# A four-layer graph network in one kernel: the product of probabilities and v is taken for four row tiles at once

## The chip, the cores and the metric

The kernel runs on one core of a Trainium2 chip. The metric is the time of one execution on the device in microseconds (us); lower is better. A core has five engines that work beside each other and wait for each other by semaphores: TensorE (PE in the profile: matrix products, weights are loaded by PEld beside the products), VectorE (DVE), ScalarE (ACT), GpSimd (POOL) and SyncE (SP), which here only issues DMA transfers. Each engine works through its own list of instructions in a fixed order.

## The reference

Inputs are 32 graphs of 512 nodes with 256 features each and a 512x512 adjacency matrix of zeros and ones. Four layers follow; each is `x = layernorm(x + layer(x))`, in fp32:

```python
# layer 0: attention with 8 heads of 32 columns, masked by adj
q, k, v = heads(x @ Wq + bq), heads(x @ Wk + bk), heads(x @ Wv + bv)
scores = where(adj > 0, q @ k.T / sqrt(32), -9e15)
x = layernorm(x + (softmax(scores) @ v) @ Wo + bo)
# layer 1: h = (1 + eps) x + adj @ x, two dense layers with relu
x = layernorm(x + relu(h @ W1 + b1) @ W2 + b2)
# layer 2: g = eps x + adj @ x, dense to 1024, rmsnorm, silu, dense back
x = layernorm(x + silu(rmsnorm(g @ W1 + b1) * w) @ W2 + b2)
# layer 3: normalised graph Laplacian of layernorm(x), softplus
xn = layernorm3(x) * gamma + beta
x = layernorm(x + softplus(xn @ W_self + (L @ xn) @ W_neigh))
```

## The kernel before

**Tiling.** A graph (a "batch", index b) has NT = 4 row tiles of 128 nodes and DC = 2 chunks of 128 features. The eight heads form two groups g of HPG = 4 heads, so that a group fills 128 rows of q and k transposed (qT, kT). `graph(b)` (L508) records every operation of one batch: which engine, a planned cost, what it reads, writes and holds. Nothing is issued while recording.

**Attention.** `qk(m)` (L693) computes qT and kT of one head group. `attend(g)` (L762) then goes over the four row tiles t. For each it computes the scores of four heads (L776, four small products in four strips of 32 rows of the array), adds the mask and takes the row minimum on DVE (L800), and takes the exponential on ACT (L814). The probabilities `pq` must be transposed before they can be multiplied with v. For batches after the first, DVE transposes 32x32 blocks in place (L850), four DMAs write the tile to a DRAM buffer `via` (L862, 256 KB each), and one DMA reads it back in the transposed arrangement as `pT` (L874, 1 MB). The first batch (`early`) transposes on PE instead. The product with v, called pv (L893), uses four strips of 32 columns of the array and adds into one PSUM bank `po_att`. It is one operation for two row tiles: after t = 1 and after t = 3, so two operations for a head group and four for a batch. There are three buffers for `pT` and four for `via`. After pv the sums are divided out (`normalise`, L946) and the output weights Wo are applied (`pair_sum`, L980, written `po<-wo,oT`).

**The other stages**, by the names that the profile shows: `ph` (L1170) is the product of adjacency and x, `pa` and `pg` (L1187) are the first dense layers of layer 1 and 2, `po<-w,aT` and `po<-w,gT` (L991) their second ones, `pz` (L1436) and `pa_l` (L1478) are layer 3. Between them stand layernorms, whose reciprocal root is a small POOL operation (L1044). Small bf16 or narrow products spread row factors: `pm_t` (L934), `pr_r` (L963), `pm` (L1281), `pb` (L1314).

**Buffers that the change touches.** x is loaded into its own tile `x_sb` (one buffer, L573); POOL then writes x plus the bias of Wo into `y_att` (L683), the tile of the residual (two buffers). `kT` holds both head groups (two buffers, L689). In layer 2, ACT squares each of eight chunks into `sq` (two buffers, L1263), which POOL adds up (L549).

**What sets the order of the work.** The order is planned before anything is issued. Class `Order` (L60) simulates all engines with the planned costs and, at each step, lets an engine take the operation with the smallest key among those that can start soon (`run`, L108). A key is `b * PERIOD` plus a due time: a mix of the earliest and the latest start (`LATE`) plus a constant for the stage (`LEAD`); the last batch's keys are shifted by `HASTE`. Choosing an operation that needs another division of the PE array ("whole", "row" for scores, "col" for pv) adds `TURN_DUE` to its key. So work of three or four batches is interleaved, and from the third batch on the order repeats with each batch. All DMAs are issued by SP in the planned order; a DMA that waits holds up those behind it.

Of the kernel before, what the change touches and what calls it, by code (L numbers as in the profile page):

```python
# [9 lines left out]
F32 = mybir.dt.float32  # L10
# [9 lines left out]
RMS_EPS = 1e-6  # L20
HEADS = 8

PERIOD = 65998
LEAD = {
    "adjT": 17900, "agg1": -34100, "agg2": -112800, "degree": 46800, "diag": 80200,
    "lap": -5300, "ln0": -81400, "ln1": -47100, "ln2": 88600, "ln3": -37200, "load": -92700,
    "move": 7000, "pv": 8000, "pz": 22200, "qk": 5800, "rinv": -8800, "rms": -91800,
    "scores": -5600, "silu": 57000, "softplus": -39900, "v": -32400, "w11": -49700,
    "w12": -36000, "w21": 10500, "w22": -22500, "wo": 21900, "x3T": -21500, "xT": 67600,
}  # L30


# [27 lines left out]
class Order:  # L60
# [9 lines left out]
    TABLE, TABLE_DUE = 1300, 9000  # L70

    TURN = {"whole": 93, "row": 290, "col": 150}
    TURN_DUE = 500
    LATE = 0.09
    HASTE = 137

    def __init__(self):
        self.ops = []
# [204 lines left out]
def kernel(  # L283
# [117 lines left out]
    def load_x(b, t):  # L401
        nc.sync.dma_start(t(), x[b].rearrange("(t p) d -> p t d", p=P))
# [105 lines left out]
    def graph(b):  # L508
# [13 lines left out]
        def pe(cost, fn, r, w, *hold, turn="whole"):  # L522

            op([("PE", cost, fn, {"turn": turn})], r, w, hold)
# [44 lines left out]
        def small(name, bufs=2, shape=None):  # L569
            return Buf(sb, shape or [P, NT], F32, "s_" + name, f"{name}_{b}", bufs)  # L570


        xs = Buf(sb, [P, NT, D], F32, "x_sb", f"x_{b}", 1)  # L573
        ad = Buf(sb, [P, NT, N], F32, "adj_sb", f"adj_{b}", 1)
        op(
            [("SP", 4000 if first else 8100, lambda: load_x(b, xs), {"issue": 1500 if first else 560, "lat": 300})],
            [], [(xs,)],
        )
        op(
            [("SP", 6000 if first else 8900, lambda: load_adj(b, ad), {"issue": 3000 if first else 560, "lat": 300})],  # L580
# [73 lines left out]
        if early:  # L654
            for c in range(DC):
                pt = bank("pt")

                def tr_x(c=c, pt=pt):
                    for t in range(NT):
                        nc.tensor.transpose(  # L660
                            pt[:, t * P : (t + 1) * P], xs[:, t, c * P : (c + 1) * P], ident
                        )

                pe(460, tr_x, [(xs,)], [(pt,), ("begun", c)], xT)
                evacuate(lambda c=c: xT[:, c, :], pt, [(pt,)], [(xT, c)])
        else:
            for q in range(4):
                op(
                    [("SP", 4900, lambda q=q: load_blocks(xT(), x[b], q), {"issue": 660, "lat": 300})],
                    [("begun", c) for c in range(DC)], [(xT, c, q) for c in range(DC)],  # L670
                )
            dve(
                1200,
                lambda: nc.vector.transpose(
                    xT().rearrange("p c i -> p (c i)"), xT().rearrange("p c i -> p (c i)")
                ),
                [], [(xT, c, q) for c in range(DC) for q in range(4)]
                + [(xT, c) for c in range(DC)],
            )
        y = tmp([P, NT, D], "y_att", 2)  # L680
        pool(
            2400,
            lambda: nc.gpsimd.tensor_tensor(y(), xs(), rows(bo_r), ALU.add),  # L683
            [(xs,), ("bo",)], [(y, t) for t in range(NT)],
        )


        qT = tmp([P, DC, N], "qT", 1)
        kT = tmp([P, DC, N], "kT", 2)  # L689
        v = tmp([P, NT, D], "v", 2)  # L690
        xTc = [(xT, c) for c in range(DC)]

        def qk(m):  # L693
            stage[0] = "qk"
            for w, w_k, dst, bias_c, bias_k, scale in (
                (wq, "wq", qT, bqs_c, "bqs_c", QK_SCALE),
                (wk, "wk", kT, bk_c, "bk_c", 1.0),
            ):
                pq = bank("pq")

                def mm(w=w, pq=pq):
                    for c in range(DC):
                        nc.tensor.matmul(  # L703
                            pq(),
                            lhsT=w[:, c, m * P : (m + 1) * P],
                            rhs=xT[:, c, :],
                            start=(c == 0),
                            stop=(c == DC - 1),
                        )

                pe(1720, mm, xTc + [(w_k,)], [(pq,)], dst)
                to = lambda dst=dst: dst[:, m, :]
                src = pq
                if dst is kT and not early:
                    to = lambda: kT[:, m, :].rearrange("p (a c s) -> p c a s", a=4, c=4)
                    src = lambda pq=pq: pq().rearrange("p (c a s) -> p c a s", a=4, c=4)
                col = bias_c[:, m : m + 1]
                either(
                    [(pq,), (bias_k,)], [(dst, m)],
                    (  # L720
                        750,
                        lambda to=to, src=src, col=col, scale=scale: nc.vector.tensor_scalar(
                            to(), src(), scalar1=scale, scalar2=col,
                            op0=ALU.mult, op1=ALU.add,
                        ),
                    ),
                    (
                        680,
                        lambda to=to, src=src, col=col, scale=scale: nc.scalar.activation(
                            to(), src(), AF.Identity, bias=col, scale=scale  # L730
                        ),
                    ),
                )
# [28 lines left out]
        def attend(g):  # L762
# [5 lines left out]
            for t in range(NT):  # L768
# [4 lines left out]
                def mm(t=t, sc=sc):  # L773
                    for j in range(HPG):
                        hp = slice(j * HD, (j + 1) * HD)
                        nc.tensor.matmul(  # L776
                            sc[:, j, :],
                            lhsT=qT[hp, g, t * P : (t + 1) * P],
                            rhs=kT[hp, g, :],
                            start=True,  # L780
                            stop=True,
                        )

                pe(
                    870, mm, [(qT, g), (kT, g)], [(sc, j) for j in range(HPG)], mx,
                    turn="row",
                )

# [33 lines left out]
                    )  # L822
                stage[0] = "move"

                pT = tmp([P, 4, HPG, NT, 32], "pT", 3)
                pTs.append(pT)
                if early:
                    for j in range(HPG):
# [18 lines left out]
                else:  # L847
# [7 lines left out]
                    )  # L855


                    via = Buf(dr, [4, 32, 4, HPG * NT * 32], F32, "via", f"via_{b}", 4)

                    def away(pq=pq, via=via):  # L860
                        for i in range(4):
# [18 lines left out]
                        [(via,)], [(pT, a) for a in range(4)],  # L880
                    )

                if t % 2 == 0:
                    continue
                stage[0] = "pv"
                two = [(t - 1, pTs[t - 1]), (t, pT)]

                def pv(two=two):

                    for t, pT, c in [(t, pT, c) for t, pT in two for c in range(NT)]:  # L890
                        for j in range(HPG):
                            h = g * HPG + j
                            nc.tensor.matmul(  # L893
                                po[j * HD : (j + 1) * HD, t * P : (t + 1) * P],
                                lhsT=v[:, c, h * HD : (h + 1) * HD],
                                rhs=pT[:, :, j, c, :],
                                start=(c == 0),
                                stop=(c == NT - 1),
                            )

                pe(
                    1780, pv,
                    [(pT, a) for _, pT in two for a in range(4)] + [(v, c) for c in range(NT)],
                    [(po,)], oT, turn="col",
                )

# [230 lines left out]
        x1 = y  # L1137


        def residual(xin, bias_r, bias_k):  # L1140
            r = tmp([P, NT, D], "y", 3)
            pool(
                2400,
                lambda: nc.gpsimd.tensor_tensor(r(), xin(), rows(bias_r), ALU.add),
                [(xin, t) for t in range(NT)] + [(bias_k,)], [(r, t) for t in range(NT)],
            )
            return r

# [49 lines left out]
        stage[0] = "agg1"  # L1198
        set_diagonal(self1, "self1")
        hT = aggregate(x1)  # L1200
        r1 = residual(x1, b12_r, "b12_r")
        set_diagonal(self2, "self2")
        stage[0] = "w11"
        aT = tmp([P, C1, N], "aT", 1)
# [31 lines left out]
        for m in range(C2):  # L1236
# [16 lines left out]
            if m == 0:  # L1253
                act(
                    630,
                    lambda m=m: nc.scalar.activation(ssq(), gT[:, m, :], AF.Square),
                    [(gT, m)], [(ssq,)],
                )
            else:
                sq = tmp([P, N], "sq", 2)  # L1260
                act(
                    630,
                    lambda m=m, sq=sq: nc.scalar.activation(sq(), gT[:, m, :], AF.Square),  # L1263
                    [(gT, m)], [(sq,)],
                )
                add_to(ssq, sq, 1280, 690, [(sq,)], [(ssq,)])
# [235 lines left out]
        for rt in row_tiles:  # L1502
# [6 lines left out]
            s_ = lambda part=part: sp[:, part]  # L1509
            z_ = lambda part=part: zy[:, part, 0:D]  # L1510
            x_ = lambda part=part: x3[:, part]
            act(cost, lambda s_=s_, z_=z_: nc.scalar.activation(s_(), z_(), AF.Abs), z0, spk)
            act(
                cost,
                lambda s_=s_: nc.scalar.activation(s_(), s_(), AF.Exp, scale=-1.0), [], spk,
# [75 lines left out]
```

## Time and profile before

The page gives shares of the whole span; the stretch that counts is the repeating one.

| | |
|---|---|
| median of 3 runs | 3356.13 us (3354.51 to 3359.38) |
| profiled execution, its own time | 3356.19 us |
| its span from first to last instruction | 3354.4 us (1.8 us lie around it) |
| granted TensorE clock, mean | 0.996 |
| one batch in the repeating stretch, 1496.98 to 1599.11 us | 102.13 us |
| busy in that stretch | PE 102.13, DVE 88.09, ACT 58.76, POOL 26.61 us; DMA share 0.81 |

A busy PE in this table means that a product was in flight or modelled to be; the starts of the products, not their modelled ends, tell how fast they follow each other. The idle time that a group of instructions shows is followed by what ended it. For a DMA the page gives the median from issue to landing.

### The profile page before, as it was taken

To read this page: it belongs to the slowest core of one execution; us is meant where nothing else is said; L and a number is where in the kernel's file an instruction comes from. 1 tells how busy PE (TensorE), PEld (TensorE's weight loads), DVE (VectorE), ACT (ScalarE), POOL (GpSimd) and SP (SyncE) were. 2 spreads that over 40 slices of the span, in tenths; PEclk is the share of its full clock that TensorE was granted. 3 is DMA by queue.
4 is the path that set the end of the run, shared out by engine and by line. 5 is a ranking of instruction groups with operands and counts; after the bars stand their busy time and mean duration, and the time that the engine had idled before them with its cause. 6 is when DMAs were issued, how large, how long until landed. Compare 5 with 4: busy or idle time off the path is not lost.

```text
span 3354.4 us, 55143 instructions
## 1 busy us (share of the span) xinstructions
PE 3305.2 (99%) x19624; PEld 1980.2 (59%) x19624; DVE 2823.6 (84%) x6412; ACT 1887.3 (56%) x3863; POOL 843.4 (25%) x610
## 2 busy tenths in 40 slices
PE   8999999999999999999999999999999999999997
PEld 5556655566565566565666655665655665556654
DVE  7878888888888888888888888888888888888855
ACT  6555565565655655655555655555656556556533
POOL 1222222322222322222222223222222222232221
PEclk9999999999999999999999999999999999999999
DMA  5878878778878787787787787787887887877820
GB/s 143 246 235 216 207 200 222 226 202 211 204 202 234 204 220 197 206 219 226 201 215 207 202 228 214 208 210 201 215 232 199 214 206 201 225 224 183 206 53 13
DMA packets 768195, 677.23 MB, mean 202 GB/s; under 512 B 540208, under 2 KB 592304, under 8 KB 736176
## 3 DMA queue, kind: packets, MB, share of 16 engines
q1 hardware_dynamic: 767920, 673.71, 76.5%
q8 instruction: 155, 2.54, 0.3%
q14 instruction: 120, 0.98, 0.1%
HBM read 380.52 MB, written 293.08 MB: 201 GB/s over the span
## 4 chain that ended last, share of the span: by engine, by line
PE 96%; DVE 1%; ACT 1%; DMA 1%; issue 0%; POOL 0%; SPq 0%; POOLq 0%; DVEq 0%; ACTq 0%
PE po L991 23%; PE ph L1170 13%; PE pg L1187 13%; PE sc L776 8%; PE po_att L893 7%; PE pz L1436 7%; PE pa_l L1478 7%; PE pa L1187 7%; PE pq L703 6%; PE pv L744 3%; ACT pq L814 0%; PE pr_r L963 0%; PE pb L1314 0%; DVE pq L800 0%; DMA via<-pq 0%
## 5 line engine op out<-in xcount | busy, mean ns | idle before, releaser
L814 ACT ACTIVATE pq<-pq,mx 128x512 f32<-128x512 f32 x1024 | 729.0, 714 | 333.3 <-DVE mx L800 265.7
L800 DVE CUSTOM_DVE_ANT_0 pq<-sc,bias 128x512 f32<-128x512 f32 x1024 | 664.3, 685 | 42.3 <-PE sc L776 23.7
L850 DVE STREAM_TRANSPOSE pq<-pq 128x2048 f32<-128x2048 f32 x248 | 567.9, 2296 | 6.4 <-ACT pq L814 6.4
L1187 PE MATMUL pg<-hT,w 128*128 128x512 f32 x1024 | 480.3, 603 | 2.0 <-DVE gT L1242 2.0
L991 PE MATMUL po<-w,gT 128*128 128x256 f32 x2048 | 451.3, 381 | 6.3 <-ACT gT L1341 6.3
L991 PEld LDWEIGHTS po<-w,gT 128*128 128x128 f32 x2048 | 391.3, 191 | 62.1 <-ACT gT L1341 7.1
L549 POOL TENSOR_TENSOR ssq<-ssq,sq 128x512 f32<-128x512 f32 x217 | 276.9, 1276 | 521.6 <-ACT sq L1263 521.2
L1187 PEld LDWEIGHTS pg<-hT,w 128*128 128x128 f32 x1024 | 184.6, 190 | 251.0 <-issue 238.1
L776 PE MATMUL sc<-kT,qT 32*128 32x512 f32 x2048 | 291.9, 640 | 3.0 <-DVE mx L800 3.0
L893 PEld LDWEIGHTS po_att<-pT,v 128*32 128x32 f32 x8192 | 216.3, 110 | 99.1 <-issue 49.2
L893 PE MATMUL po_att<-pT,v 128*32 128x128 f32 x8192 | 251.2, 275 | 5.5 <-DMA pT<-via 5.5
L1478 PE MATMUL pa_l<-zy,adjT 128*128 128x256 f32 x1024 | 243.0, 385 | 0.0
L1044 POOL TENSOR_TENSOR rstd<-ve,nhalf 128x4 f32<-128x4 f32 (+1 forms) x132 | 135.6, 1028 | 422.5 <-DVE ve L1039 417.5
L1242 DVE TENSOR_SCALAR gT<-pg,b_c 128x512 f32<-128x512 f32 x187 | 140.3, 751 | 120.0 <-PE pg L1187 119.9
L549 POOL TENSOR_TENSOR sp<-sp,y 128x1024 f32<-128x1024 f32 x31 | 73.4, 2367 | 657.7 <-ACT sp L1528 644.7
L1436 PE MATMUL pz<-wsn,xnT 128*128 128x512 f32 x512 | 236.9, 606 | 0.7 <-ACT sq L1263 0.6
L1170 PE MATMUL ph<-adjT,y 128*128 128x512 f32 x512 | 227.0, 596 | 4.7 <-ACT y L1070 4.7
L1170 PE MATMUL ph<-adjT,y_att 128*128 128x512 f32 x512 | 228.2, 598 | 0.0
L1187 PE MATMUL pa<-hT,w 128*128 128x512 f32 x512 | 228.1, 598 | 0.0
L991 PE MATMUL po<-w,aT 128*128 128x256 f32 x1024 | 226.5, 379 | 0.0
L991 PEld LDWEIGHTS po<-w,aT 128*128 128x128 f32 x1024 | 194.3, 190 | 28.0 <-ACT aT L1218 0.8
L1478 PEld LDWEIGHTS pa_l<-zy,adjT 128*128 128x128 f32 x1024 | 189.3, 190 | 29.9 <-issue 0.7
(165 smaller groups left out, 4896.3 us busy)
## 6 DMA issues: line engine op xcount, KB each, us to landing
via<-pq SPq DMA_DIRECT2D x992, 256.0 KB, 4.4
pT<-via SPq DMA_DIRECT2D x248, 1024.0 KB, 6.4
adj<-in_adj_dram SPq DMA_DIRECT2D x32, 1024.0 KB, 7.9
adjT<-in_adj_dram SPq DMA_DIRECT2D x124, 256.0 KB, 6.0
x<-in_x_dram SPq DMA_DIRECT2D x32, 512.0 KB, 6.1
xT<-in_x_dram SPq DMA_DIRECT2D x124, 128.0 KB, 5.9
x3d<-y SPq DMA_DIRECT2D x31, 512.0 KB, 3.9
xnT<-x3d SPq DMA_DIRECT2D x124, 128.0 KB, 3.7
```

The source lines that it names most:

```text
L549: lambda: nc.gpsimd.tensor_tensor(dst(), dst(), src(), ALU.add), {},
L703: nc.tensor.matmul(pq(), lhsT=w[:, c, m * P : (m + 1) * P], rhs=xT[:, c, :], start=(c == 0), stop=(c == DC - 1),)
L776: nc.tensor.matmul(sc[:, j, :], lhsT=qT[hp, g, t * P : (t + 1) * P], rhs=kT[hp, g, :], start=True, stop=True,)
L800: lambda t=t, j=j, sc=sc, row=row: nc.vector.tensor_tensor_reduce(out=row(), in0=sc[:, j, :].rearrange("p (a n) -> p a n", a=4), in1=bias[ ...
L814: lambda t=t, j=j, row=row: nc.scalar.activation(row(), row(), AF.Exp, bias=mx[:, t, j : j + 1], scale=-1.0, accum_out=rs[:, g, t, j : j + 1],
L850: lambda pq=pq: nc.vector.transpose(pq().rearrange("p a j c s -> p (a j c s)"), pq().rearrange("p a j c s -> p (a j c s)"),),
L893: nc.tensor.matmul(po[j * HD : (j + 1) * HD, t * P : (t + 1) * P], lhsT=v[:, c, h * HD : (h + 1) * HD], rhs=pT[:, :, j, c, :], start=(c == 0),
L991: nc.tensor.matmul(po[:, i * D : (i + 1) * D], lhsT=lhs[:, k, t * P : (t + 1) * P], rhs=w[:, k, :], start=(i == 0 and k == 0), stop=(i == ...
L1170: nc.tensor.matmul(ph(), lhsT=xin[:, m, c * P : (c + 1) * P], rhs=adjT[:, m, :], start=(m == 0), stop=(m == NT - 1),)
L1187: nc.tensor.matmul(pa(), lhsT=w[:, c, m * P : (m + 1) * P], rhs=hT[:, c, :], start=(c == 0), stop=(c == DC - 1),)
L1436: nc.tensor.matmul(pz(), lhsT=xnT[:, c, t * P : (t + 1) * P], rhs=wsn[:, c, :], start=(c == 0), stop=(c == DC - 1),)
L1478: nc.tensor.matmul(pa[:, i * D : (i + 1) * D], lhsT=adjT[:, m, t * P : (t + 1) * P], rhs=zy[:, m, D : 2 * D], start=(m == 0), stop=(m == N ...
```

## The change

The product of probabilities and v becomes one operation for all four row tiles of a head group, recorded after the last of them (t = 3). It needs all four `pT` tiles at once, so there are four `pT` buffers, and eight `via` buffers. To make room, x is loaded straight into `y_att`, where POOL adds the bias in place; `x_sb` is gone; `kT` becomes one tile for each head group with three buffers; `sq` has one buffer. Two keys are added that order operations only in the plan: the residual of layer 1 comes after the softplus of two batches before. The constants of the plan (period, leads, price of a turn) are other ones, so that the order of the work changes everywhere.

```diff
-PERIOD = 65998
+PERIOD = 63146
 LEAD = {
...
-    TURN_DUE = 500
-    LATE = 0.09
-    HASTE = 137
+    TURN_DUE = 1750
+    LATE = 0.17
+    HASTE = -6727
...
-        xs = Buf(sb, [P, NT, D], F32, "x_sb", f"x_{b}", 1)
+        y = tmp([P, NT, D], "y_att", 2)
...
-            [("SP", 4000 if first else 8100, lambda: load_x(b, xs), {...})],
-            [], [(xs,)],
+            [("SP", 4000 if first else 8100, lambda: load_x(b, y), {...})],
+            [], [(y, t) for t in range(NT)],
...
-        y = tmp([P, NT, D], "y_att", 2)
         pool(
             2400,
-            lambda: nc.gpsimd.tensor_tensor(y(), xs(), rows(bo_r), ALU.add),
-            [(xs,), ("bo",)], [(y, t) for t in range(NT)],
+            lambda: nc.gpsimd.tensor_tensor(y(), y(), rows(bo_r), ALU.add),
+            [("bo",)], [(y, t) for t in range(NT)],
         )
...
-        kT = tmp([P, DC, N], "kT", 2)
+        kTs = [tmp([P, N], "kT", 3, f"kT{g}") for g in range(DC)]
...
-                            rhs=kT[hp, g, :],
+                            rhs=kTs[g][hp, :],
...
-                pT = tmp([P, 4, HPG, NT, 32], "pT", 3)
+                pT = tmp([P, 4, HPG, NT, 32], "pT", 4)
...
-                    via = Buf(dr, [4, 32, 4, HPG * NT * 32], F32, "via", f"via_{b}", 4)
+                    via = Buf(dr, [4, 32, 4, HPG * NT * 32], F32, "via", f"via_{b}", 8)
...
-                if t % 2 == 0:
+                if t < NT - 1:
                     continue
                 stage[0] = "pv"
-                two = [(t - 1, pTs[t - 1]), (t, pT)]
-
-                def pv(two=two):
-
-                    for t, pT, c in [(t, pT, c) for t, pT in two for c in range(NT)]:
+
+                def pv():
+
+                    for t, c in [(t, c) for t in range(NT) for c in range(NT)]:
                         for j in range(HPG):
                             h = g * HPG + j
                             nc.tensor.matmul(
                                 po[j * HD : (j + 1) * HD, t * P : (t + 1) * P],
                                 lhsT=v[:, c, h * HD : (h + 1) * HD],
-                                rhs=pT[:, :, j, c, :],
+                                rhs=pTs[t][:, :, j, c, :],
...
                 pe(
-                    1780, pv,
-                    [(pT, a) for _, pT in two for a in range(4)] + [(v, c) for c in range(NT)],
+                    3500, pv,
+                    [(pT, a) for pT in pTs for a in range(4)] + [(v, c) for c in range(NT)],
                     [(po,)], oT, turn="col",
                 )
...
-        r1 = residual(x1, b12_r, "b12_r")
+        r1 = residual(x1, b12_r, "b12_r", [("sp", b - 2)])
...
-                sq = tmp([P, N], "sq", 2)
+                sq = tmp([P, N], "sq", 1)
...
-            act(cost, lambda s_=s_, z_=z_: nc.scalar.activation(s_(), z_(), AF.Abs), z0, spk)
+            act(
+                cost, lambda s_=s_, z_=z_: nc.scalar.activation(s_(), z_(), AF.Abs), z0,
+                spk + [("sp", b)],
+            )
```

## The prediction

> **What bounds the kernel now.** I read the page's engine shares and its chain first, then PE's own waits, then PE's timeline in a repeating stretch. The page:
>
> ```profile
> PE 3305.2 (99%) x19624; PEld 1980.2 (59%) x19624; DVE 2823.6 (84%) x6412; ACT 1887.3 (56%) x3863; POOL 843.4 (25%) x610
> PE 96%; DVE 1%; ACT 1%; DMA 1%; issue 0%; POOL 0%; SPq 0%; POOLq 0%; DVEq 0%; ACTq 0%
> L893 PE MATMUL po_att<-pT,v 128*32 128x128 f32 x8192 | 251.2, 275 | 5.5 <-DMA pT<-via 5.5
> pT<-via SPq DMA_DIRECT2D x248, 1024.0 KB, 6.4
> ```
>
> PE is busy for 99% of the span and 96% of the chain that ended last lies on it. Does it ever wait? The list of PE's waits:
>
> ```profile
> PE po L991 <- ACT gT L1341: 6.3, 2, 4.8
> PE po_att L893 <- DMA pT<-via: 5.5, 1, 5.5
> PE ph L1170 <- ACT y L1070: 4.7, 2, 2.7
> PE pt L1379 <- DVE y L1062: 4.3, 1, 4.3
> ```
>
> Each occurs once or twice in 32 batches: at the start or in the last two batches. In the repeating stretch PE waits for nothing, one batch takes 102.13 us, and the time is what PE needs to issue its list. So only a shorter list, or a new wait, moves the time. What a piece costs is read from start to start, not from the modelled durations:
>
> ```profile
> 1568.99 1.88 PE L703 MATMUL pq<-xT,wk 128*128 128x512 f32 x4
> 1570.71 1.88 PE L1187 MATMUL pg<-hT,w 128*128 128x512 f32 x4
> 1572.52 1.14 PE L776 MATMUL sc<-kT,qT 32*128 32x512 f32 x8
> 1573.59 5.42 PE L1187 MATMUL pg<-hT,w 128*128 128x512 f32 x12
> 1578.94 1.96 PE L893 MATMUL po_att<-pT,v 128*32 128x128 f32 x64
> 1580.82 5.42 PE L1436 MATMUL pz<-wsn,xnT 128*128 128x512 f32 x12
> 1586.08 0.29 PE L1281 MATMUL pm<-red,quad 128*128 128x16 f32 x2
> ```
>
> Four whole products of 512 columns take 1.72 us (1568.99 to 1570.71), so 0.429 each; four that precede scores take 1.81: 0.09 more. The twelve between scores and pv take 5.35 instead of 5.15, and the twelve after pv 5.26. So one visit to the divided array costs 0.20 us beside its own work: 0.09 going in, 0.11 coming back. Scores that are followed at once by pv take 1.07 us all the same, so a pair costs 0.20 once. A pv of two row tiles takes 1.88 us. What of that is start-up shows near the beginning, where one is cut in half by a wait:
>
> ```profile
> 151.54 1.08 PE L893 MATMUL po_att<-pT,v 128*32 128x128 f32 x32
> 158.13 1.94 PE L893 MATMUL po_att<-pT,v 128*32 128x128 f32 x32 [5.51 <-DMA pT<-via]
> ```
>
> 32 products have the duration 1.08 and 64 have 1.96, so 32 more cost 0.88.
>
> **The change, part by part.** Counts are from the instruction order of the changed kernel, which can be listed without running it; PE has the same 10566 program instructions in both.
>
> *Pv in one operation.* 128 operations become 64. One of four tiles takes 1.88 + 2 x 0.88 = 3.64 us against 2 x 1.88 = 3.76: 0.12 saved, 64 x 0.12 = 7.7 us.
>
> *Fewer visits to the divided array* (pv merged, dearer turn, new leads). Unbroken runs of scores and pv fall from 295 to 258: 37 x 0.20 = 7.4 us. In a repeating batch it is nine against eight.
>
> *Small products at new places.* `pm` now stands before scores in 28 batches; before, it stood between two `pz`, and took 0.14 us to issue with the four `pz` after it 0.08 slow. `pm_t` of the sums now precedes scores in 30 batches, against `pg` 0.05 slow after it before. If scores hide all of that, 28 x 0.19 + 30 x 0.06 = 7.1 us go; if their turn costs come on top, nothing. The nearest row, `pm_t` before scores near the start (0.14 from start to start), shows it half hidden; I take 3.5. Work of PE: -18.6 us, between -15.1 and -22.2.
>
> The Trainium skill ("TensorEngine Tiling (Array Packing)", Key Properties) says that changing the tiling mode drains TensorE, but not a change of tile alone. The trace shows 0.20 for a visit and no visible extra between scores and pv, two different modes. By the rule every such pair would have a third drain; at 0.1 each, 28 pairs fewer (88 to 60) would add some 3 us to the gain.
>
> *Four `pT` held until pv ends.* No load of the next group's `pT` can land earlier: what is late next is the four loads that SP issues after a pv. Summing PE's prices in the new order, the second pv of a batch stands 19.0 us after the end of the first (pz, scores, `po<-wo`, `pa_l`, scores). What do four loads need? Two issued 0.9 us apart (1.23 less one issue of 0.34) land after 6.2 and 7.8 us, 2.5 apart:
>
> ```profile
> 1544.28 1.23 SPq L874 DMA_DIRECT2D pT<-via  x2
> DMA to landing us min/median/max: 6.2/7.0/7.8
> DMA to landing us min/median/max: 4.6/6.4/9.9
> ```
>
> (The last line is over all 248.) So 0.3 + 6.4 + 3 x 2.5 = 14.2 us; with the longest landing 17.7. Spare: 4.8, at worst 1.3 us. Cost 0. If the cover goes, PE stands and with it everything, once in each batch. The `via` writes are done in time: scores of that group lie 30 us or more ahead. The other pv comes 75 us after its predecessor.
>
> The Trainium skill ("Trainium Kernel Development and Optimization", Best Practices) asks for double buffering, so that transfers run beside compute. It speaks against this: a fourth buffer that is consumed with the other three leaves none to load ahead. By it the loads would be exposed; by the rows 19.0 us of other products cover them.
>
> *At the start* that cover is missing: between the pv of the second batch stand only 6.4 us of PE, against 14.2: a wait of 7.8 us, where before there was one of 5.5: +2.3.
>
> *x into `y_att`.* Same bytes, same POOL operation (2.38 us). The load now waits on SP for PE and POOL to let go of `y_att` of two batches before, at the end of the first aggregation; the queue behind it holds `via` and `pT` transfers needed over 20 us later. Landing takes 6.1 us and the addition 2.4; behind it in POOL's list stands the root of layer 1's layernorm, asked for about 20 us after the load can start: spare 11 us. Cost 0; if that cover were gone, PE would wait for the second aggregation.
>
> *`kT` by group, `sq` with one buffer.* A `kT` tile is written again some 80 us after the last scores that read it: 0. A square (0.63) and its addition on POOL (1.28) can no longer overlap, 2.1 us with two hand-overs for each of seven chunks, where `pg` come every 1.72 plus two or three scores between them. The chain ends some 2 us later; `pm` comes 10.2 us after the last `pg` instead of 7.2: 0. The two order keys add no instruction and no wait of their own.
>
> *New order, new slacks.* Tightest is layernorm 1, from the last `po<-w,aT` to the second `ph`. Before, 6.6 us of PE covered it and the normalised rows were ready 0.9 us early. Now 6.4 us cover it (three `pq`, `pm_t`, scores), and DVE first does three masks and a 2.3 us transpose of probabilities. Summing DVE's list from the start of that `po` (reductions until 2.6, masks 4.2, reciprocal 4.4, transpose 6.7, two additions 7.9, statistics 10.2, root on POOL 11.5, two rows 12.4) against 13.3 leaves 0.9 us. The same sum for the transposed adjacency (four loads landed 9.6 us after `pa_l` ends) leaves 1.4 us. Cost 0, bound 0.5 for a batch. DVE's total falls by some 9 us in the run, since more copies went to ACT.
>
> *At the end* layernorm 1 of the last but one batch is covered by `pm_t` and `pr_r` alone (0.5 us) instead of scores and pv (2.96): its wait of 1.94 becomes 4.4, +2.4. From the first aggregation of the last batch on, the order is the same.
>
> Sum: -18.6 + 2.3 + 2.4 = -13.9 us. Against the profiled execution's 3356.2 (its own time; the median is 3356.1, the same) that is **3342 us**.
>
> **Rivals.** A: small recurring waits. Layernorm 1 or the adjacency misses its slack by 0.2 to 0.5 us in 29 repeating batches: +6 to +15, so 3348 to 3357. For: slacks of about a microsecond on a DVE that is 86% busy. Against: before ran with 0.9 and no wait.
>
> B, the other side: `pT` loads late for the second pv. It decides from where four loads take 19.6 us instead of 14.2 (the spare 4.8 and some 0.6 saved in a batch), that is 4.3 us from one to the next instead of 2.5. At the mean rate of the run (202 GB/s, 5.2 us for 1 MB) they would take 22.3: 3.3 us of stall, x 29 = +96, 3438 us. For: DMA share 0.81. Against: loads issued together follow at 2.5 us even so.
>
> C: no change that counts. Turns are saved but PE waits for them elsewhere, since another engine or the loop from batch to batch holds 102.1: 3354 to 3358. Against: DVE, the next, needs 88 of 102.
>
> **How the numbers follow.** Forecast 72%; its own range takes work of -15 to -22 and start and end waits of 0 to +9: 3333 to 3350. A 14%, B 7%, C 4%, a wait that I have not seen 3%. The range 3333 to 3353 takes in most of A. About 0.2% (6.7 us) is what a measurement tells from no change, so faster is below 3349.4: the forecast and half of A, 0.79. Same: half of A and C, 0.11. Slower: B and the unseen, 0.10.
>
> **What would show it.** One batch near 101.6 us; 64 pv groups of 128 products, 3.6 us from start to start; PE's list of waits still made of single events, with `po_att` near 8 us at one place; `ph` after layernorm 1 without a recurring wait. Wrong: `po_att <- pT` or `ph <- ACT y` some 29 times, or a batch of 102.1 us with a new idle engine before PE.

## The result and the profile after

| | before | after |
|---|---|---|
| median | 3355.56 us | 3401.3 us (3398.24 to 3405.35) |
| ratio | | 1.0135, 95% interval [1.0117, 1.0153] |
| span of the profiled execution | 3354.4 us | 3400.9 us |
| granted TensorE clock, mean | 0.996 | 0.993 |

The change makes the kernel slower by 46 us; 14 us less was forecast. The lines of the page that answer to those shown of the kernel before:

```profile
PE 3305.0 (97%) x19624; PEld 1992.9 (59%) x19624; DVE 2751.4 (81%) x6338; ACT 1897.9 (56%) x3936; POOL 843.0 (25%) x610
PE 69%; DMA 12%; SPq 11%; DVE 5%; issue 2%; ACT 1%; DVEq 0%; POOL 0%; POOLq 0%; ACTq 0%
L895 PE MATMUL po_att<-pT,v 128*32 128x128 f32 x8192 | 238.3, 274 | 4.6 <-DMA pT<-via 4.6
pT<-via SPq DMA_DIRECT2D x248, 1024.0 KB, 7.8
```

PE fell from 99% of the span to 97%. The chain that ended last no longer lies on PE alone: 28% of it is transfers, SP's queue and DVE. A `pT` load lands after 7.8 us in the median instead of 6.4. Who makes PE wait is in the list of PE's waits (total us, times, longest us):

```profile
PE pv L747 <- DVE xT L677: 27.3, 24, 2.8
PE sc L779 <- DVE mx L803: 9.2, 5, 5.2
PE ph L1172 <- issue: 7.5, 25, 2.1
PE po_att L895 <- DMA pT<-via: 4.6, 3, 3.0
PE pz L1438 <- DVE gT L1244: 4.2, 1, 4.2
```

The first and the third come in most batches, once in each: the products that make v (`pv<-wv,xT`, not the pv of this change) wait for the transposed x, and `ph` behind them again. The list of before has no line of this kind. The wait for `pT` at the second pv of a batch, rival B, is absent: 4.6 us in three events, all near the start.

Where the 46.5 us of span lie, by the starts of the first `ph` of each batch (us):

| stretch | before | after | difference | by the forecast's terms |
|---|---|---|---|---|
| to the fourth batch | 393.0 | 406.7 | +13.7 | about +1 |
| one of the next 26 batches | 102.13 | 103.39 | +1.26 | -0.6 |
| these 26 | 2655.5 | 2688.2 | +32.7 | -15 |
| the rest | 305.9 | 305.9 | 0 | about +1 |

The chain of one repeating stretch says what stands behind the wait. Its pieces in order of time (start us, us, what):

```profile
1709.17 3.68 PE po_att L895 x128
...
1713.59 9.13 DMA pT<-via
1722.71 0.02 issue
1722.73 5.61 SPq L590
...
1728.39 2.20 SPq L590
...
1735.23 7.37 DMA adjT<-in_adj_dram
...
1745.10 2.19 DVE pq L853
1747.29 1.14 DVE xT L677
1748.42 0.04 issue
1748.47 3.72 PE pv L747 x16
```

A pv ends and lets go of four `pT` at once. Four loads of 1 MB start between 1712.36 and 1716.01 us; a `via`, xT of a later batch and the transposed adjacency (both L590) follow. The last load of the adjacency lands at 1742.60. For 3.95 us until then DVE stands, with the transposes of probabilities and of xT behind it in its list. DVE and PE in that stretch (the bracket is the idle time before, and what ended it):

```profile
1742.72 2.37 DVE L624 STREAM_TRANSPOSE adjT<-adjT 128x1024 f32<-128x1024 f32 x2 [3.95 <-DMA adjT<-in_adj_dram]
1745.02 2.27 DVE L853 STREAM_TRANSPOSE pq<-pq 128x2048 f32<-128x2048 f32 x1
1747.21 1.20 DVE L677 STREAM_TRANSPOSE xT<-xT 128x1024 f32<-128x1024 f32 x1
```

```profile
1727.05 3.72 PE L1480 MATMUL pa_l<-zy,adjT 128*128 128x256 f32 x16
1730.70 1.14 PE L779 MATMUL sc<-kT,qT 32*128 32x512 f32 x8
1735.72 12.03 PE L993 MATMUL po<-w,gT 128*128 128x256 f32 x55
1748.47 3.72 PE L747 MATMUL pv<-wv,xT 128*128 128x256 f32 x16 [0.71 <-DVE xT L677]
1752.42 4.10 PE L1172 MATMUL ph<-adjT,y_att 128*128 128x512 f32 x9 [0.23 <-issue]
```

The adjacency's tile comes free when `pa_l` ends (1730.8). Before, its last load landed 10.2 us after that (median of 25 batches, 9.3 to 11.1); after the change 12.1 us (10.8 to 13.9). The delay is there already when the loads are started: the last of the four starts 6.0 us after `pa_l` ends instead of 4.0, and from its start to its landing it takes 6.2 us against 6.1 (medians). SP's rows for xT and the adjacency, first before, then after:

```profile
1693.12 4.30 SPq L589 DMA_DIRECT2D xT<-in_x_dram  x3
1700.26 5.52 SPq L589 DMA_DIRECT2D adjT<-in_adj_dram  x4
```

```profile
1720.29 11.01 SPq L590 DMA_DIRECT2D xT<-in_x_dram  x4
1731.40 6.96 SPq L590 DMA_DIRECT2D adjT<-in_adj_dram  x4
```

Part of that is a wait of SP's own. Each transfer raises one of eight semaphores when it has landed, and the four loads of xT have the same four semaphores as the four of `pT` ahead of them: an xT load is not started before its `pT` load has landed (the second one landed at 1722.71, and the second xT load starts at 1722.73). From 400 to 3000 us SP's list of waits has this line; that of before has none like it:

```profile
SPq L590 <- DMA pT<-via: 62.3, 46, 3.3
```

The windows of the changed kernel (busy time of each engine, then granted clock, DMA share, GB/s) show what the transfers do meanwhile:

```profile
1720.00:1724.00 4.00, 4.00 (x20) 3.51 (x20) 3.83 (x12) 2.78 (x9) 0.00 (x0) 1.00 1.03 422
1736.00:1740.00 4.00, 4.00 (x20) 3.54 (x19) 2.78 (x9) 3.95 (x6) 0.00 (x0) 1.00 1.20 116
```

From 1712 to 1744 us the DMA share is 1.02 in the mean: the transfer engines are busy through the whole stretch, first with `pT` at 422 GB/s, then with the adjacency in pieces of 128 bytes at 116. (The share is reckoned from the packets' own times and can pass 1.)

### The profile page after: what moved, and what is told of

It reads as the page before. It is cut to its first block, busy times and chain, and to the rows that moved or that the text cites. A ratio compares the mean times of both kernels' runs of the same rounds, so it can differ in the third digit from the quotient of the medians.

```text
span 3400.9 us, 54937 instructions
## 1 busy us (share of the span) xinstructions
PE 3305.0 (97%) x19624; PEld 1992.9 (59%) x19624; DVE 2751.4 (81%) x6338; ACT 1897.9 (56%) x3936; POOL 843.0 (25%) x610
## 4 chain that ended last, share of the span: by engine, by line
PE 69%; DMA 12%; SPq 11%; DVE 5%; issue 2%; ACT 1%; DVEq 0%; POOL 0%; POOLq 0%; ACTq 0%
PE ph L1172 13%; PE pg L1189 13%; PE po L993 10%; SPq L590 10%; PE pq L706 6%; DMA pT<-via 6%; PE sc L779 6%; PE pa L1189 6%; DMA adjT<-in_adj_dram 4%; PE po_att L895 4%; PE pz L1438 4%; PE pv L747 3%; PE pa_l L1480 2%; DVE pq L853 2%; DVE adjT L624 1%
## 5 line engine op out<-in xcount | busy, mean ns | idle before, releaser
L803 DVE CUSTOM_DVE_ANT_0 pq<-sc,bias 128x512 f32<-128x512 f32 x1024 | 654.3, 682 | 39.0 <-PE sc L779 23.3
L1189 PE MATMUL pg<-hT,w 128*128 128x512 f32 x1024 | 460.7, 598 | 0.0
L895 PE MATMUL po_att<-pT,v 128*32 128x128 f32 x8192 | 238.3, 274 | 4.6 <-DMA pT<-via 4.6
L1328 DVE SCALAR_TENSOR_TENSOR gT<-gT,rw_c,pb 128x512 f32<-128x512 f32 x256 | 171.3, 742 | 35.0 <-PE pb L1316 35.0
L817 ACT ACTIVATION_READ_ACCUMULATOR pq<-pq,mx 128x1 f32 x1024 | 191.9, 187 | 0.0
```

What stands on the lines that cost most here:

```text
L803: lambda t=t, j=j, sc=sc, row=row: nc.vector.tensor_tensor_reduce(out=row(), in0=sc[:, j, :].rearrange("p (a n) -> p a n", a=4), in1=bias[ ...
L817: lambda t=t, j=j, row=row: nc.scalar.activation(row(), row(), AF.Exp, bias=mx[:, t, j : j + 1], scale=-1.0, accum_out=rs[:, g, t, j : j + 1],
L895: nc.tensor.matmul(po[j * HD : (j + 1) * HD, t * P : (t + 1) * P], lhsT=v[:, c, h * HD : (h + 1) * HD], rhs=pTs[t][:, :, j, c, :], start=( ...
L1189: nc.tensor.matmul(pa(), lhsT=w[:, c, m * P : (m + 1) * P], rhs=hT[:, c, :], start=(c == 0), stop=(c == DC - 1),)
```

## The experiments

Theory T1 after the first look: the four loads that one pv sets free crowd the transfers, the adjacency lands late and DVE hands the wait on. Rivals: T2, DVE's list is too long there, whatever the transfers; T3, PE's own products cost more in the new order.

**1. The same loads in long rows.** xT and the transposed adjacency are loaded in rows of 4 and 8 KB instead of pieces of 128 bytes: the same bytes, the same operations behind them.

```diff
...
-    load_blocks(adjT(), adj[b], q)
+    load_plain(adjT(), adj[b], q)
...
-    load_blocks(xT(), x[b], q)
+    load_plain(xT(), x[b], q)
```

> The changed kernel with the rows of xT and of the transposed adjacency loaded as they lie (packets of 4 and 8 KB) instead of gathered in blocks (packets of 128 B): same bytes, same order, same instructions. The arrangement of x and adjacency for the products is left out, so the values are others. Theory T1 (the adjacency lands late for VectorE, because the burst of four pT loads, via, xT and the adjacency go through one queue at the same time): the wait of pv on the transposed xT goes, a batch takes 101.5 to 101.8 us, the span is 3355 to 3368. Rival T2 (VectorE's list from the Laplacian to the second aggregation is too long, whatever the loads do): the wait stays, a batch keeps 103.4 and the span 3395 or more. Rival T3 (PE's own list is dearer than its prices say): waits go, a batch still takes over 102.5.

Measured: 3352.41 us (one run; the kernel before on the same chip 3357.51). A batch takes 101.65 us in the mean of 26, and from 400 to 3000 us PE's list of waits is empty. T1 holds: with cheaper transfers the waits go, and DVE's list and PE's order are as they were, so T2 and T3 fall. The adjacency now lands 7.5 us after `pa_l` ends (median, 6.7 to 8.8).

PE's list is the same here as in after, instruction by instruction, so the two can be laid on each other. Over the 26 batches after takes 45.3 us more, and all of it lies in three places: 31.1 in front of `pv<-wv,xT`, 5.6 between its products, 8.7 between it and `ph`. Everything else differs by hundredths of a microsecond. This kernel also shows PE's prices without a wait:

```profile
1680.96 3.70 PE L901 MATMUL po_att<-pT,v 128*32 128x128 f32 x128
1684.59 3.70 PE L1444 MATMUL pz<-wsn,xnT 128*128 128x512 f32 x8
1688.13 0.29 PE L1289 MATMUL pm<-red,quad 128*128 128x16 f32 x2
1688.35 1.14 PE L785 MATMUL sc<-kT,qT 32*128 32x512 f32 x8
```

A merged pv takes 3.63 us from start to start; 3.64 was forecast. `pm` before scores takes 0.22, as much as its 0.14 and 0.08 before: scores hide nothing of it.

**2. Half of each pT.** Each `pT` load brings half of the tile, and pv takes one of its four blocks four times.

```diff
-    pT().rearrange("p i j c s -> p (i j c s)"), via().rearrange("a p i e -> (a p) (i e)")
+    pT()[:, 0:2].rearrange("p i j c s -> p i (j c s)"), via()[:, :, 0:2].rearrange("a p i e -> (a p) i e")
...
-    rhs=pTs[t][:, :, j, c, :]
+    rhs=pTs[t][:, 0:1, j, c, :].to_broadcast([P, 4, 32])
```

> The changed kernel with half of each pT loaded (512 KB instead of 1 MB), and pv reading one of the four blocks four times: same products, other values; half of the probabilities' way back is left out. T1 with the burst as the cause: the four loads take 5 us of the queue instead of 10, the adjacency lands some 2 us or more earlier, the wait of pv on xT goes, a batch takes 101.5 to 102, the span is 3355 to 3375. T2: no change, 3395 or more.

Measured: 3359.71 us (one run), 102.06 us for a batch, the adjacency 10.8 us after `pa_l`. So the bytes of `pT` count, and not only the pieces of 128 bytes. This kernel moves fewer of them everywhere, not in the burst alone; that their timing matters, and not their sum, follows from the kernel before, which moves as many as after. Kernels 1, 2 and after have the same order of work, so their batches can be laid on one curve: from the end of `pa_l` to the landing of the adjacency, and from the same end to the next `ph` (us, from the records of single batches):

| kernel | landing -> `ph` |
|---|---|
| long rows | 6.7 -> 20.4; 7.7 -> 20.4; 8.8 -> 20.4 |
| half of pT | 10.0 -> 20.4; 10.6 -> 20.4; 11.0 -> 20.8; 12.0 -> 21.8 |
| after | 10.8 -> 20.6; 11.9 -> 21.7; 12.4 -> 22.2; 12.9 -> 22.7; 13.8 -> 24.6 |

PE reaches `ph` after 20.4 us as long as the adjacency lands within 10.6; beyond that each microsecond costs a microsecond. Two of the 25 batches of after lie about 1 us above that line, the last one of the table among them. In both the granted TensorE clock stood at half for 3.4 us from the products behind the wait on (0.72 in the window from 1540 to 1546 us), which the repeating batches of the kernel before and of kernels 1 and 2 never show.

**3. xT's transpose ahead of the adjacency's on DVE.** In 23 batches DVE transposes xT, which has long landed, before it waits for the adjacency.

```diff
...
+            if ad and 6 <= b < 29:
+                out.remove(tr[0])
+                out.insert(ad[0], tr[0])
...
```

> The changed kernel with one VectorE instruction moved in 23 of the batches: the transpose of xT stands before that of the adjacency, where VectorE is idle for 4 us. T1: xT has landed some 9 us before the adjacency, so pv no longer waits for it, and what hangs on the adjacency is 1.1 us shorter: a batch takes 101.6 to 102.2, the span is 3365 to 3380. T2: the same work is only done in another order, the second aggregation waits instead: 3390 or more.

Measured: 3378.76 us, ratio 1.0062 [1.0046, 1.0079]; a batch 102.43 us, a little over what T1 gave it. The adjacency lands as late as in after (median 12.0). More than half of the loss in a batch goes; what stays has moved one product on, by PE's waits from 400 to 3000 us:

```profile
PE ph L1203 <- ACT v L573: 10.3, 7, 1.9
PE ph L1203 <- issue: 2.9, 9, 0.6
PE pv L778 <- DVE xT L708: 2.6, 3, 1.1
```

**4. xT's loads ahead of the burst.** As 3, and SP issues the four xT loads before the last `via` and the four `pT` loads.

```diff
...
+                for o in ld:
+                    out.remove(o)
+                j = out.index(before)
+                out[j:j] = ld
...
```

> As the kernel with the moved transpose, and the four loads of xT ahead of the last via before the burst of pT loads, where SP idles. T1: the small packets of xT are out of the way when the adjacency is issued, which lands 1 to 3 us earlier; a batch takes 101.5 to 101.7, the span is 3360 to 3370, some 10 us better than the moved transpose alone at most. T2: no better than the moved transpose alone. If the burst of pT alone delays the adjacency, no better either.

Measured: 3614.93 us, ratio 1.0768 [1.0752, 1.0784]: a miss, far off. The waits of SP's queue from 700 to 3000 us, and those of PE, name it:

```profile
SPq L621 <- PE pz L1469: 286.6, 21, 13.7
```

```profile
PE pa_l L1511 <- ACT zy L1496: 173.5, 21, 9.2
```

The tile of xT comes free only at `pz`, so SP stands up to 13.7 us in front of these loads, and the `via` behind them starts late. The reductions wait for that `via` (a `pq` buffer), and `pa_l` in the end for ACT. In each of the 23 batches the granted clock also fell to half for 10.2 us (in one, from 1728.7 us on, within a wait that ends at 1734.2), which is worth some 2.4 of the 10 us by which such a batch is longer than in kernel 3. The adjacency does land earlier, 10.7 us after `pa_l` in the median, as T1 had it, but in a batch so much longer that this settles nothing on the burst. A load moved ahead in an in-order queue also moves its wait.

**5. The adjacency's loads from ACT's queue.**

```diff
...
-    nc.sync.dma_start(dst[32 * q : 32 * q + 32]...
+    queue.dma_start(dst[32 * q : 32 * q + 32]...
...
-    load_blocks(adjT(), adj[b], q)
+    load_blocks(adjT(), adj[b], q, nc.scalar)
...
```

> The changed kernel, with the four loads of the transposed adjacency started from ACT's queue instead of SP's, at the same place of the order. Theory Q (the loads come late because they stand in SP's in-order queue behind pT, via and xT): each batch's loads start when pa_l ends, land 9.6 us later or sooner as in the kernel before, and a batch takes 101.7 to 102.0 us: 3352 to 3360 us. Theory B (the sixteen engines have too many bytes to move in that stretch, whoever asks): the loads still land 11 us or more after pa_l ends, a batch stays at 102.8 to 103.8 and the time at 3385 to 3410 us. If ACT itself is held up by starting them, the wait moves to what ACT makes (rows of v, exponentials) and the batch becomes longer than 103.4.

Measured: 3578.06 us (one run), 109.31 us for a batch. The loads land 14.3 us after `pa_l` (median), later than from SP's queue. A piece of its chain:

```profile
1813.15 0.60 ACTq L590
...
1815.65 4.96 ACTq L590
...
1820.68 5.92 DMA adjT<-in_adj_dram
```

Theory Q falls: out of SP's queue the first load starts 0.04 us after `pa_l` ends instead of 0.7, and the last lands later all the same. Theory B has the loads right and the batch wrong; the third case came, ACT held up by its starts. The four of this batch occupied ACT for 9.75 us, and the last of them comes 8.0 us after the first (medians: 5.2 in after). That only the bytes hold the loads is therefore argued, not shown, by this run. The Trainium skill ("DMA: Bandwidth & Descriptors", Issuing engines are not separate DMA queues) states that transfers of all issuing engines run on the same 16 DMA engines and interleave, so that another issuer saves only issue time. Here it did not save that either: one start instruction occupied ACT for 4.96 us.

Of the 5.9 us that a batch takes more than in after, some 2.2 are the later landing. The granted clock is behind part of the rest: it stood at half for 120 us in these 26 batches, 4.6 in each, which is worth up to 2.3 us of a batch.

**6 and 7. Another order, planned with the transfers' own prices.** The planner knows one price for each transfer, as if it ran alone. In these kernels it has one shared transfer resource, and the leads (with the price of a turn and the other constants of the plan) are fitted to that.

```diff
...
+            if "dma" in way[3] and not back:
+                dma_free = max(dma_free, t) + way[3]["dma"]
+                o.t1 = max(t + cost, dma_free + self.FLIGHT)
+                free[e] = max(free[e], dma_free - self.BACKLOG)
...
-                            {"issue": 600, "lat": 300},
+                            {"issue": 600, "lat": 300, "dma": 2500},
...
```

> The changed kernel's operations in another order: the planner is told that transfers share one resource (2.5 us for a pT, 3.2 for a via, 0.8 for each xT load, 1.9 for each load of the transposed adjacency, 2.2 of flight, and SP held once 6 us lie ahead), and leads are fitted to that. The two pv of a batch then stand 59 and 36 us apart instead of 19 and 75, and there are 287 visits to the divided array instead of 258. Theory (the merged pv and its prices are right, only the order crowds the transfers): no recurring wait, a batch of 101.67 + 0.2 = 101.9 us, the third batch still 5 us long, in all 3342 to 3358 us. Rival (four pT let go at once always cost a wait, whatever the order): a recurring wait of 0.5 us or more, batch 102.4 or more, 3365 us or more.

Measured: 3360.31 us, ratio 1.0007 [0.9997, 1.0016]. Repeating batches take 101.82 us without a recurring wait, as the theory had it; the stretch to the fourth batch takes 401.7 and the fourth 106.8, and with that the time lies just above the range given.

> The same planner with other leads, in which the two pv of a batch stay close, 20 and 74 us apart as in the changed kernel, with the masks, transposes and adjacency loads placed by the shared resource. 283 visits to the divided array. If the closeness of the two pv is itself the cause (four pT, via, xT and adjacency in one stretch of 30 us), the adjacency still lands 11 us or more after pa_l ends and a batch takes 102.5 us or more: 3375 us or more. If only what DVE and the queue do around it matters, a batch takes 101.7 to 102.0 and the run 3345 to 3362 us.

Measured: 3353.75 us, ratio 0.9985 [0.9975, 0.9994]; 101.56 us for a batch. The two pv stay 20 us apart, so closeness alone is not the cause. In kernel 6 the adjacency lands 12.4 us after `pa_l`, no sooner than in after, and none of its batches pays for it; in 7 it lands after 10.8, and the batches that go over about 11.2 pay some tenths (101.56 in the mean, 101.48 in most). DVE and PE of kernel 7:

```profile
1805.95 2.30 DVE L859 STREAM_TRANSPOSE pq<-pq 128x2048 f32<-128x2048 f32 x1
1809.85 2.37 DVE L630 STREAM_TRANSPOSE adjT<-adjT 128x1024 f32<-128x1024 f32 x2 [1.60 <-DMA adjT<-in_adj_dram]
1812.14 1.20 DVE L683 STREAM_TRANSPOSE xT<-xT 128x1024 f32<-128x1024 f32 x1
```

```profile
1815.30 1.03 PE L753 MATMUL pv<-wv,xT 128*128 128x256 f32 x4
1817.89 2.32 PE L1178 MATMUL ph<-adjT,y_att 128*128 128x512 f32 x5
```

DVE still stands 1.60 us, but the transpose of probabilities goes before the wait instead of after it, and only a quarter of the products that make v stands before `ph`. So the cause in after is both: the burst makes the adjacency late, and the order left 0.4 us between its usual landing (10.2) and the kink (10.6). That the lateness goes with the merged pv, and not with one order, is borne out by all the orders tried: with the loads as they were and merged pv the medians are 12.1 (after), 12.4, 10.8 and 11.6 (kernels 6, 7 and 8), with pv two by two 10.2 in the kernel before and in kernel 9.

**8 and 9. What the merged pv is worth.** 8 is 7 with leads fitted further; 9 is the kernel before (pv of two row tiles) under the same planner, its leads fitted in the same way.

> Four row tiles in one pv, planner with the shared resource, the leads fitted further from those of the last run: the two pv of a batch still 20 us apart, visits to the divided array 256 instead of 283. Theory (PE's list sets the time once nothing waits in the repeating stretch, and a visit costs 0.20 us): 0.9 visits fewer in a batch, so 101.48 less 0.18 = 101.3 us, no recurring wait, 3345 to 3351 us. Rival (the fitted order has used up what DVE and the transfers leave, and the gain on paper turns into new waits): batch 101.5 to 102.3, 3352 us or more.

> The kernel before (pv of two row tiles, x in its own tile, three pT) with the same planner and leads fitted to it in the same way: 270 visits to the divided array instead of 295. It tells what of the gain is the planner's alone. Theory (pv in one operation saves 0.12 us each, the rest are visits): 0.9 visits fewer than before in a batch, 102.13 less 0.18 = 101.95 us, 3346 to 3356 us, and slower than the merged pv under the same planner by 0.24 us in a batch for pv alone, 0.2 for each visit more. Rival (the merged pv is worth nothing, the planner is worth everything): a batch of 101.5 us or less, 3347 us or less.

| kernel | time, ratio to before | to the fourth batch | one of the next 26 | the rest |
|---|---|---|---|---|
| 7, merged | 3353.75 us, 0.9985 [0.9975, 0.9994] | 396.3 | 101.56 | 310.5 |
| 8, merged | 3353.14 us, 0.9988 [0.9979, 0.9997] | 402.9 | 101.71 | 304.8 |
| 9, two by two | 3353.11 us, 0.9987 [0.9978, 0.9996] | 392.2 | 101.96 | 309.0 |

Kernel 9 came out as the price of a visit says: 102.13 - 25/30 x 0.2 = 101.96. Kernel 8 missed its theory, and its mean and its time lie where the rival put them: most batches take 101.47, no less than the 101.48 of kernel 7, with 0.9 visits fewer, and some wait. The visit that kernel 7 has more stands before a small product that interrupts `pa_l` anyway:

```profile
1689.15 1.14 PE L785 MATMUL sc<-kT,qT 32*128 32x512 f32 x8
1690.22 0.22 PE L942 MATMUL pm_t<-ident_b,rmsp 128*12 128x128 bf16 x1
1690.37 1.99 PE L1486 MATMUL pa_l<-zy,adjT 128*128 128x256 f32 x8
```

Scores take their 1.07 and `pm_t` its 0.15 there, as elsewhere. So the visit shares the price of an interruption that is there anyway, and comes nearly free. PE's records bear that out: in one repeating batch the whole products are interrupted, by visits or small products or both together, 10 times in 7 and in 8, and take 84.35 and 84.34 us; in the kernel before 13 times and 84.82, in kernel 9 11 times and 84.52. No run tries it by itself. Under like planners the merged pv saves 0.25 to 0.4 us in a repeating batch, 6 to 11 us in 26, and its start is 4 to 11 us longer: the three times cannot be told from each other. All three lie some 0.1% below before, less than the 0.2% that was named as the least measurable for a single comparison; their intervals, from 10 or 11 runs each, end just short of 1.

## Why the prediction was wrong

- **The step that failed** is in the part on new order and new slacks: "The same sum for the transposed adjacency (four loads landed 9.6 us after `pa_l` ends) leaves 1.4 us. Cost 0, bound 0.5 for a batch." The landing came from one batch of the kernel before, where no four `pT` loads stand ahead. Its own median was 10.2, and in the changed kernel it was 12.1. With a landing of 9.6 there is 1.0 us of room by the kink at 10.6, so the sum over DVE's list was about right (1.4); the input was not. It cost 103.39 - 101.65 = 1.74 us for a batch instead of 0, all of it at `pv<-wv,xT` and the `ph` behind it.
- **Four `pT` held until pv ends.** As its own step it held: the last of the four landed at 1727.75, 14.9 us after pv ended (14.2 forecast), and the next pv began at 1731.77. But the step asked only whether pv would wait. The same 4 MB delayed everything behind them, and the cost came out in the row for the adjacency. That the loads share the engines was used for rival B and not for the slacks. That SP would stand before the xT loads until the `pT` loads had landed was in no sum.
- **PE's list.** Merged pv 3.63 us (3.64 forecast). A batch without waits 101.65 (near 101.6 forecast): 0.48 us less than before, where 0.58 was forecast and 0.47 by its lower bound. Scores directly in front of a pv take 1.07 us in kernel 1 too (1679.89 to 1680.96), so the change from one division of the array to the other shows no extra there either. The visits' price carried over to kernels 6 and 9, but not to 7 and 8, which are faster than it says. The small products gave nothing for `pm`, at the lower bound of that term. Its sum was also off by itself: it takes 0.19 us for each `pm` where its own rows give 0.14 + 0.08 = 0.22.
- **Start.** +2.3 was forecast for one wait for `pT`; the stretch to the fourth batch grew by 13.7. PE waited 4.6 us for `pT` there, but also 4.2 at `pz` and 5.2 at a score. What is behind the wait at `pz` shows in DVE's records of the third batch:

```profile
253.09 0.69 DVE L803 CUSTOM_DVE_ANT_0 pq<-sc,bias 128x512 f32<-128x512 f32 x1 [5.08 <-DMA via<-pq]
```

  A reduction waits 5.08 us for a `via` to leave its `pq` buffer, the copies of `pg` stand behind it, and `pz` behind those. The step named what the four loads wait for and not what waits behind them in SP's queue. With half of each `pT` (kernel 2) this stretch took 397.9, with long rows (kernel 1) 401.2, so cheaper transfers take away 8.8 and 5.5 of the 13.7. In this stretch the granted clock stood at half for 13.7 us in after and 6.8 before, worth up to 3.4 us more. The rest was not taken apart.
- **End.** The rest after the thirtieth `ph` is 305.9 us in both; the forecast, +2.4 less what PE saves there, was near +1.
- **x into `y_att`, `kT`, `sq`, layernorm 1.** None of them stands among the recurring waits of PE, as forecast.
- **Rivals.** A was the right mechanism with the right name, the adjacency missing its slack, and a price of 0.2 to 0.5 us that the runs put at 1.74: it was bounded by the slack, not by how far a burst can move the landing. B, the second pv waiting for its loads, did not happen. C fell with kernel 1, where 101.65 us is reached.

## What to carry to other kernels

When a change lets several buffers go at once, the loads that follow come as one burst, and the question is not only whether their own consumer waits: every later transfer in that stretch lands later, and its consumer's slack must be summed with that landing. A landing time read in the trace of before holds only for the traffic that stood ahead of it there; take its spread over the batches, and add the bytes that the change puts in front. A slack on an in-order engine is best tested by laying landing against consumer over many batches: the kink tells how much room there was.

## What the runs showed of the hardware

- **A start instruction can be slow itself.** With the burst ahead, the second xT load (1024 pieces of 128 bytes) kept SP for 5.61 us (median of all batches 4.85); in long rows the same starts took about 0.3. It takes no merged pv: in the kernel before the fourth xT load kept SP for 2.96 us in the median, in kernel 9 the third for 5.16.
- **Small pieces take longer than long rows of the same bytes.** The adjacency's four loads of 256 KB landed about 2 us apart in after (1736.11 to 1742.60) and 1.2 apart in long rows. The Trainium skill ("DMA: Bandwidth & Descriptors", Specifications) puts the least transfer for line rate at 512 bytes; pieces of 128 against rows of 8 KB agree with that in direction.
- **`pT` loads in a burst land one behind the other at a fixed distance**: the four landed 2.5, 2.7 and 2.4 us after each other (1720.21, 1722.71, 1725.37, 1727.75), as two did in the trace of before (2.5).
- **The granted TensorE clock can fall to half behind a wait of about 2 us, and need not.** In after this happened in two of 25 repeating batches, for 3.4 us each, at waits of 2.02 and 2.65 us; the longest wait, 2.83 us, shows nothing of it. In kernel 5, whose waits go up to 5.5 us, it happened 31 times in 26 batches.
